# Where four weight pieces land, and in which order the last products run, in a four-layer attention and feed-forward kernel

## The chip, the core and the metric

The kernel runs on one core of one Trainium2 chip. The metric is the device time of one execution in microseconds (us); the time before is the median of four runs. A core has five engines, each with an instruction stream of its own: PE (TensorE, matrix products), DVE (VectorE), ACT (ScalarE), POOL (GpSimd) and SP (SyncE). SP, and for some transfers ACT and POOL, issue the DMAs. [...] PE reads SBUF and writes PSUM, the accumulator memory; DVE and ACT read results from there.

## The reference, cut to what matters

The input `x` has 4 batches of 256 tokens of 256 numbers, in float32. Four layers follow; each adds a cross-attention on 512 context tokens, and then a feed-forward part:

```python
x = x + xattn_L(layernorm(x), ctx)       # L = 1..3: 16 heads of 128, 8 kv heads
x = x + ffn_L(layernorm(x))
# layer 1's ffn: 8 experts of width 176, each token goes to 2, and a shared expert
# layer 3's ffn, for each batch b:
weights = x @ W_r + b_r                           # one number for each token
topk_vals, topk_idx = top_k(weights, 64)
h   = gelu(x[topk_idx] @ W1 + b1)                 # 64 tokens, 256 -> 1024
blk = h @ W2 + b2                                 # 1024 -> 256
out = scatter(blk * weight) + x * (not selected)
```

Before an attention layer the raw weights Wq, Wk, Wv and Wo are folded, head by head, into two matrices: `m_sb` (Wq with Wk) and `n_sb` (Wv with Wo). Attention then works with these and with the context directly.

## The kernel before, in words

`bounded_path` runs once. PE, ACT, DVE and POOL execute what they are given in the order in which the program is written by hand (`manual_schedule`), so a wait at one instruction holds all that stands behind it on that engine. SP's DMAs are also issued in written order.

**The raw weights of layer 2.** `load_raw(L, i, after)` (line 958) issues four DMAs on SP for piece `i` of 4: `wq` and `wo` of 512 KB, `wk` and `wv` of 128 KB. They land in tiles of the pool `rawp`, which here has 3 buffers. `after` makes each DMA wait for a given instruction. `folding` (line 974) is a generator of eight steps, two for each piece. A step is four products `pm` (L983), one product `pn` (L999), ACT's scaling into `m_sb` (L991) and two squares (L994), and DVE's copy into `n_sb` (L1002). `pm` and `pn` take turns in the PSUM buffers called "mm".

**Around it: layer 1's experts.** Tokens are sorted into 23 blocks of 128 slots. For a block, POOL gathers tokens from DRAM (`xg`), PE turns them and multiplies (`pgu`, `pgT`, `pyr`), ACT copies the result (`yr`, L2315), and SP writes it to DRAM (`yd`, L2316). In the loop over `j`, pieces 0, 1 and 2 of layer 2's weights are issued at `j` = 2, 8 and 14, each behind the `yr` copy of the block just finished. After the loop `load_raw(2, 3)` asks for piece 3. It takes the buffers of piece 0, and so waits until PE has read them in the first two fold steps. Then come the rest of the shared expert (`psh`, `pysh`), the eight fold steps, and `Back`: 16 gathers by POOL (`yg`, L2325), two for each half batch, of which 12 are issued in a row and four later; DVE adds them to `x` (L2333). Layer 2's first queries (`pq`, L1765) follow.

**The last output of an attention layer.** For the last batch, `last_output` (line 1889) multiplies head pairs 4 to 7 with `n_sb`, in one PSUM tile `py` of 2 chunks of 128 tokens (L1896): 16 products, 32 entries of the trace, head pair outside, chunk inside. DVE then adds both chunks to `x` (L1904). The four head pairs are divided by their softmax sums just before, two on POOL and two on DVE (L1860). DVE also finishes the other half of the output (`w`, L1793 to L1796, and L1887) before L1904. After it come `Norm` (L917 to L920: statistics on DVE, a power on POOL) and the feed-forward part.

**The end.** Layer 3's feed-forward part routes each batch in stages (`Router`: `weights`, `spread`, `places`, `gathered`, `rest`). `rise3` computes `ph` and the gelu (L2697, L2704), `fall3` computes `po` (L2712) and `blk` (L2716), and `put(b)` sends a batch's 64 rows back to their tokens (`py`, L2722), adds them (L2726) and issues the output (L2727). `blk` holds two batches on its 128 partitions: rows 0 to 63 are the even batch, rows 64 to 127 the odd one. Batches 0 to 2 are raised together, the last one for itself.

Of the kernel before, what the change touches and what calls it, by code (L numbers as in the profile page):

```python
# [9 lines left out]
F32 = mybir.dt.float32  # L10
# [3 lines left out]
ALU = mybir.AluOpType  # L14
# [3 lines left out]
P = 128  # L18
B, S, D = 4, 256, 256
NC = S // P  # L20
ND = D // P
SK, DC = 512, 128
NK = SK // P
H, G = 16, 8
# [13 lines left out]
KSEL = 64  # L38
# [797 lines left out]
def bounded_path(ctx: ExitStack, tc: tile.TileContext, t, out: bass.AP, over):  # L836
# [70 lines left out]
    class Norm:  # L907


        def __init__(self, b, name):  # L910
            self.b, self.name = b, name
            st = small.tile([P, NC, 6], F32, tag="ln_st", name=f"st_{name}")
            self.mv = small.tile([P, NC, 2], F32, tag="ln_mv", name=f"mv_{name}")
            ve = small.tile([P, NC], F32, tag="ln_ve", name=f"ve_{name}")
            self.rstd = small.tile([P, NC], F32, tag="ln_rstd", name=f"rstd_{name}")
            for c in range(NC):
                nc.vector.bn_stats(st[:, c, :], x_sb[b][:, c, :])  # L917
                nc.vector.bn_aggr(self.mv[:, c, :], st[:, c, :])
            nc.vector.tensor_scalar(ve, self.mv[:, :, 1], LN_EPS, None, ALU.add)
            nc.gpsimd.tensor_tensor(self.rstd, ve, neghalf[:, :NC], ALU.pow)  # L920
# [34 lines left out]

    raws = {}

    def load_raw(L, i, after=None):

        wq, wk, wv, wo = (t[f"L{L}_{n}"] for n in ("wqT", "wkT", "wvT", "wo"))  # L960
        h0, g0 = 4 * i, 2 * i
        wq_t = rawp.tile([P, 4, D], F32, tag="wq_t", name=f"wq_{L}_{i}")
        wk_t = rawp.tile([P, 2, DC], F32, tag="wk_t", name=f"wk_{L}_{i}")
        wv_t = rawp.tile([P, 2, DC], F32, tag="wv_t", name=f"wv_{L}_{i}")
        wo_t = rawp.tile([P, 4, D], F32, tag="wo_t", name=f"wo_{L}_{i}")
        for dst, src, a, z in ((wq_t, wq, h0, 4), (wk_t, wk, g0, 2), (wv_t, wv, g0, 2), (wo_t, wo, h0, 4)):
            dma = nc.sync.dma_start(dst, src[a * P : (a + z) * P, :].rearrange("(h e) d -> e h d", e=P))
            if after:
                behind(dma, after)
        raws[L, i] = wq_t, wk_t, wv_t, wo_t  # L970
# [711 lines left out]

    NB = S // 32 * 2

    def attention(L, m_sb, n_sb, first_xnT=None, after=None, at_end=None):

# [12 lines left out]
        with tc.tile_pool(name=f"att{L}", bufs=2) as ap:  # L1699
# [186 lines left out]
                    x = x_sb[self.b].rearrange("p c (e d) -> p (c e) d", d=P)  # L1886
                    nc.vector.tensor_tensor(x, x, w, ALU.add)  # L1887

            def last_output(b):

                py = bank("s", [P, NC, D], f"py{L}")
                for hp in range(H // 4, H // 2):
                    o = outs.pop((b, hp))
                    for c in range(NC):
                        for j in range(2):
                            nc.tensor.matmul(  # L1896
                                py[:, c, :],
                                lhsT=o[:, j * S + c * P : j * S + (c + 1) * P],
                                rhs=n_sb[:, 2 * hp + j, :],
                                start=(hp == H // 4 and c == 0 and j == 0),  # L1900
                                stop=(hp == H // 2 - 1 and c == NC - 1 and j == 1),
                            )
                for c in range(NC):
                    nc.vector.tensor_tensor(x_sb[b][:, c, :], x_sb[b][:, c, :], py[:, c, :], ALU.add)  # L1904

            xnTs[0] = first_xnT if first_xnT is not None else layernorm(0, f"a{L}_0")[1]
            first_queries(0)
# [45 lines left out]
            out.add()  # L1953
            if at_end:
                at_end()
            last_output(B - 1)

# [147 lines left out]
    with tc.manual_schedule(engines={E.PE, E.Activation, E.DVE, E.Pool}):  # L2105
        with (
# [492 lines left out]
    class Router:  # L2599


        def __init__(self, b):
            self.b = b
            self.norm = Norm(b, f"f3_{b}")

        def weights(self):
            b = self.b
# [100 lines left out]
    def fall3(i, k0, k1):  # L2708
        if k0 == 0:
            po3[i] = bank("o", [P, D], f"po3_{i}")  # L2710
        for k in range(k0, k1):
            nc.tensor.matmul(  # L2712
                po3[i], lhsT=hT[:, k, i * P : (i + 1) * P], rhs=w32[:, k, :], start=(k == 0), stop=(k == F3 // P - 1)
            )
        if k1 == F3 // P:
            nc.vector.tensor_tensor(blk[:, i, :], po3[i], b32, ALU.add)  # L2716

    def put(b):
        i, r0 = b // 2, KSEL * (b % 2)
        for c in range(NC):  # L2720
            py = bank("mm", [P, D], f"py3_{b}_{c}")
            nc.tensor.matmul(  # L2722
                py, lhsT=pickT[r0 : r0 + KSEL, i, c, :], rhs=blk[r0 : r0 + KSEL, i, :], start=True, stop=True
            )
            xc = x_sb[b][:, c, :]
            nc.vector.scalar_tensor_tensor(xc, py, wts[:, b, c : c + 1], xc, ALU.mult, ALU.add)  # L2726
            (nc.scalar if c and b >= 2 else nc.sync).dma_start(out[b, c * P : (c + 1) * P, :], xc)  # L2727

    routers = {}

# [20 lines left out]
    with tc.manual_schedule(engines={E.PE, E.Activation, E.DVE, E.Pool}):  # L2751

        pr = bank("t", [P, ND, P], "pwr")
        nc.vector.memset(ones_s, 1.0)
        for d in range(ND):
            wide = tile3b("diag", [P, NC, P], f"wr{d}")
            nc.vector.tensor_copy(wide[:, 0, :], wr[:, d : d + 1].to_broadcast([P, P]))
            nc.tensor.matmul(pr[:, d, :], lhsT=wide[:, 0, :], rhs=ident, start=True, stop=True)
        nc.vector.tensor_copy(wrb, pr.rearrange("p d q -> p (d q)"))

        def end3():
            nc.scalar.preload_act_table_set("gelu_apprx_tanh_and_others")
            routers[2].gathered()
            routers[2].rest()

        attention(3, *mn, first_xnT=xnT3, after=beside3, at_end=end3)
# [4 lines left out]
        last = Router(B - 1)  # L2771
# [95 lines left out]
```

## Time and profile before

| | |
|---|---|
| median of 4 runs | 1497.68 us |
| the four runs | 1497.06, 1490.90, 1498.69, 1498.29 us |
| the profiled execution | 1499.73 us, span 1497.5 us |
| PE busy in the span | 1453.5 us (97%) |
| DVE, POOL, ACT busy | 895.8, 663.8, 573.4 us |
| mean granted PE clock | 0.987 |

The span is the time between the first and the last record of the profiled execution; 2.2 us of its time lie around it. A line of the timeline gives a start, a length, the engine, the line of the kernel, the operation, out<-in, the shapes and a count, and in brackets how long the engine had been idle and what released it. Where several instructions are merged, the length runs from the first start to the last end. "SPq", "ACTq" and "POOLq" are an engine's instruction queue, which issues DMAs. A table of windows gives for each stretch its length, the busy time of PE, PE's weight loads, DVE, ACT and POOL with counts, the granted PE clock, the share of the DMA engines and GB/s.

### The profile page before, as it was taken

What the parts mean: (1) busy time and instruction counts of PE and PEld (TensorE: products, weight loads), DVE (VectorE), ACT (ScalarE), POOL (GpSimd) and SP (SyncE); (2) the same over time, 40 slices, a digit from 0 to 9 for tenths busy, and PEclk for the clock granted to TensorE, in tenths of its full rate; (3) what the DMA queues carried; (4) which work ended last, traced back from release to release, by engine and by line L of the source; (5) the groups of instructions that cost most, each with busy time, mean ns of one, the idle gap of its engine ahead of it and who ended that gap; (6) DMA issues with size and microseconds to landing.
All of it is one profiled execution on the core that took longest, in us unless ns stands there. A gap on an engine that the chain in (4) does not pass through costs nothing.

```text
span 1497.5 us, 19706 instructions
## 1 busy us (share of the span) xinstructions
PE 1453.5 (97%) x7287; PEld 946.0 (63%) x7287; DVE 895.8 (60%) x1940; ACT 573.4 (38%) x1100; POOL 663.8 (44%) x778
## 2 busy tenths in 40 slices
PE   8999999999999999998999999999999999999997
PEld 7665577565566666665556666665886566666666
DVE  5566774566666556522566655656445666767674
ACT  4556443433433333233543333333224433333331
POOL 2122232476555454233356556556003665455560
PEclk8899999999999999999999999999999999999999
DMA  5000031110000001154110000000310000000000
GB/s 162 2 1 2 12 95 36 67 41 0 7 1 8 1 1 50 45 175 129 43 36 1 1 1 1 1 1 0 106 36 29 31 1 1 1 0 1 1 1 31
DMA packets 40036, 43.36 MB, mean 29 GB/s; under 512 B 3897, under 2 KB 36890, under 8 KB 39932
## 3 DMA queue, kind: packets, MB, share of 16 engines
q1 hardware_dynamic: 36956, 35.85, 7.5%
q0 software_dynamic: 1872, 5.11, 1.2%
q8 instruction: 60, 0.98, 0.3%
q10 hardware_dynamic: 1104, 1.05, 0.2%
q14 instruction: 44, 0.36, 0.1%
HBM read 36.89 MB, written 5.11 MB: 28 GB/s over the span
## 4 chain that ended last, share of the span: by engine, by line
PE 90%; DVE 6%; POOL 2%; issue 1%; ACT 1%; another core or an unknown queue 0%; POOLq 0%; ACTq 0%; DVEq 0%
PE ps L1813 22%; PE po L1819 21%; PE paq L1783 5%; PE pao L1783 4%; PE pbq L1783 4%; PE pbo L1783 3%; PE ph L2476 2%; PE po L2513 2%; PE pgu L2286 2%; PE po L1329 2%; PE ps L1319 2%; PE pyf L1446 2%; PE py L1896 1%; PE paf L1396 1%; PE pn L999 1%; PE pm L983 1%
## 5 line engine op out<-in xcount | busy, mean ns | idle before, releaser
L1826 POOL TENSOR_TENSOR half<-pT 128x1024 f32<-128x1024 f32 x96 | 225.8, 2352 | 383.2 <-ACT pT L1816 333.3
L1813 PE MATMUL ps<-qT,cT 128*128 128x512 f32 x768 | 345.6, 593 | 0.4 <-ACT qT L1770 0.4
L1819 PE MATMUL po<-pT,c_sb 128*128 128x512 f32 x768 | 345.2, 592 | 0.0
L1816 ACT ACTIVATE pT<-ps,mbias 128x512 f32<-128x512 f32 x384 | 263.8, 687 | 163.9 <-PE ps L1813 153.9
L1819 PEld LDWEIGHTS po<-pT,c_sb 128*128 128x128 f32 x768 | 145.9, 190 | 183.7 <-issue 183.7
L1813 PEld LDWEIGHTS ps<-qT,cT 128*128 128x128 f32 x768 | 138.7, 190 | 138.6 <-issue 137.3
L1823 ACT COPY oT<-po 128x512 f32<-128x512 f32 x96 | 56.2, 586 | 263.6 <-PE po L1819 263.6
L1860 POOL TENSOR_TENSOR oT<-oT,wide 128x512 f32<-128x512 f32 x90 | 115.4, 1302 | 26.2 <-DVE wide L1859 26.2
L1323 ACT ACTIVATE pT<-ps 128x512 f32<-128x512 f32 x128 | 66.1, 603 | 46.5 <-PE ps L1319 46.3
L1793 DVE TENSOR_TENSOR qT<-qT,paq 128x128 f32<-128x128 f32 x90 | 25.5, 284 | 90.8 <-ACT qT L1792 90.7
L1832 DVE TENSOR_TENSOR half<-half 128x512 f32<-128x512 f32 x96 | 72.1, 751 | 10.1 <-POOL half L1826 10.1
L1834 DVE STREAM_TRANSPOSE turned<-half 128x512 f32<-128x512 f32 x96 | 68.3, 712 | 6.3
L1793 DVE TENSOR_TENSOR w<-w,pao 128x128 f32<-128x128 f32 x21 | 6.0, 286 | 109.9 <-ACT w L1792 109.9
L1783 PEld LDWEIGHTS paq<-xnT_a,m_sb 128*128 128x128 f32 x360 | 58.0, 191 | 21.5 <-PE po L1819 10.5
L1783 PE MATMUL paq<-xnT_a,m_sb 128*128 128x128 f32 x360 | 70.7, 278 | 0.1
L1783 PE MATMUL paq<-xx,m_x 128*128 128x128 f32 x360 | 69.8, 275 | 0.0
L1838 DVE TENSOR_REDUCE sums<-turned 128x16 f32<-128x512 f32 x96 | 65.9, 686 | 3.4
L1783 PE MATMUL pao<-n_x,ox 128*128 128x128 f32 x336 | 65.0, 275 | 0.0
L1859 DVE STREAM_TRANSPOSE wide<-rz 128x512 f32<-128x512 f32 x96 | 62.2, 686 | 0.1
L1792 ACT COPY qT<-paq 128x128 f32<-128x128 f32 x90 | 23.9, 265 | 85.2 <-PE paq L1783 83.1
L1796 DVE TENSOR_TENSOR qT<-qT,pbq 128x384 f32<-128x384 f32 x90 | 49.9, 554 | 9.4
L1783 PEld LDWEIGHTS paq<-xx,m_x 128*128 128x128 f32 x360 | 54.7, 192 | 0.0
(392 smaller groups left out, 2603.7 us busy)
## 6 DMA issues: line engine op xcount, KB each, us to landing
wo<-in_L_wo SPq DMA_DIRECT2D x13, 512.0 KB
wq<-in_L_wqT SPq DMA_DIRECT2D x12, 512.0 KB
yd<-yr SPq DMA_DIRECT2D x23, 128.0 KB
w<-in_F_w SPq DMA_DIRECT2D x4, 512.0 KB
wgu<-in_F_wgT SPq DMA_DIRECT2D x2, 880.0 KB
wgu<-in_F_wuT SPq DMA_DIRECT2D x2, 880.0 KB
wk<-in_L_wkT SPq DMA_DIRECT2D x12, 128.0 KB
wv<-in_L_wvT SPq DMA_DIRECT2D x12, 128.0 KB
```

The lines of the kernel that those rows point to most:

```text
L1323: nc.scalar.activation(pT[kp][:, j], ps[j], AF.Exp)
L1783: nc.tensor.matmul(p[:, at, :], lhsT=lhsT, rhs=rhs, start=(k == 0 and at == 0), stop=(k == len(of) - 1 and i == which[-1]),)
L1813: nc.tensor.matmul(ps, lhsT=cT[:, b, k * P : (k + 1) * P], rhs=qT, start=True, stop=True)
L1816: nc.scalar.activation(pT[:, k, :], ps, AF.Exp, bias=mbias[:, b, k : k + 1])
L1819: nc.tensor.matmul(po, lhsT=c_sb[:, b, k, :], rhs=pT[:, k], start=(k == 0), stop=(k == NK - 1))
L1823: done["head"] = nc.scalar.copy(raw, po).ins
L1826: nc.gpsimd.tensor_tensor(half, pT[:, 0:2], pT[:, 2:4], ALU.add)
L1832: nc.vector.tensor_tensor(part, half[:, 0], half[:, 1], ALU.add)
L1834: nc.vector.transpose(turned.rearrange("p f i -> p (f i)"), part)
L1838: nc.vector.tensor_reduce(sums[b, hp // 4][:, hp % 4, :], turned, AX.X, ALU.add)
L1859: nc.vector.transpose(wide, rzs[b, hp // 4][:, hp % 4, :, None].to_broadcast([P, NB, 32]))
L1860: eng.tensor_tensor(outs[b, hp], outs[b, hp], wide.rearrange("p f i -> p (f i)"), ALU.mult)
```

## The change

There are three groups of edits.

First, layer 2's four weight pieces are all issued within the loop over blocks, at `j` = 1, 5, 9 and 13. Piece 0 no longer lands in `rawp`, but in parts of `m_sb` and `n_sb` that belong to heads 8 to 15, which the fold writes only in its second half. Pieces 1, 2 and 3 take the three buffers, and nothing is issued after the loop.

Second, in `last_output` the chunk is the outer loop. DVE adds a chunk as soon as its eight products are there, and in layer 3 takes its statistics too (`Norm.chunk`). This holds for layers 1, 2 and 3, since all use `last_output`.

Third, the end of layer 3 is reordered: `routers[2].rest()` moves from the end of attention to behind `last.places()`; parts of `fall3(0, ...)` are put between the last batch's stages; `put` takes a pair of batches, changes between the two halves of the 128 rows from one product to the next, and uses the four "s" buffers instead of the two "mm" ones.

As built, the changed kernel has PE's first product of the second chunk wait for DVE in all three layers. In layer 1, three of the shared expert's products (`psh`) stand between the two chunks; in layers 2 and 3 nothing does.

```diff
-    def load_raw(L, i, after=None):
+    def load_raw(L, i, after=None, tiles=None):
...
-        wq_t = rawp.tile([P, 4, D], F32, tag="wq_t", name=f"wq_{L}_{i}")
-        wk_t = rawp.tile([P, 2, DC], F32, tag="wk_t", name=f"wk_{L}_{i}")
-        wv_t = rawp.tile([P, 2, DC], F32, tag="wv_t", name=f"wv_{L}_{i}")
-        wo_t = rawp.tile([P, 4, D], F32, tag="wo_t", name=f"wo_{L}_{i}")
+        if tiles is None:
+            tiles = [
+                rawp.tile(shape, F32, tag=f"{n}_t", name=f"{n}_{L}_{i}")
+                for n, shape in (("wq", [P, 4, D]), ("wk", [P, 2, DC]), ("wv", [P, 2, DC]), ("wo", [P, 4, D]))
+            ]
+        wq_t, wk_t, wv_t, wo_t = tiles
...
-                if j in (2, 8, 14):
-                    load_raw(2, j // 6, done["slots"])
-            load_raw(2, 3)
-            mn = folded(2)
+                if j == 1:
+
+                    mn = folded(2)
+                    load_raw(
+                        2, 0, done["slots"],
+                        (mn[1][:, 8:12, :], mn[0][:, 1, 12:14, :], mn[0][:, 1, 14:16, :], mn[1][:, 12:16, :]),
+                    )
+                if j in (5, 9, 13):
+                    load_raw(2, j // 4, done["slots"])
...
-            def last_output(b):
+            def last_output(b, chunk=None):
...
-                for hp in range(H // 4, H // 2):
-                    o = outs.pop((b, hp))
-                    for c in range(NC):
+                for c in range(NC):
+                    for hp in range(H // 4, H // 2):
                         for j in range(2):
                             nc.tensor.matmul(
                                 py[:, c, :],
-                                lhsT=o[:, j * S + c * P : j * S + (c + 1) * P],
+                                lhsT=outs[b, hp][:, j * S + c * P : j * S + (c + 1) * P],
                                 rhs=n_sb[:, 2 * hp + j, :],
-                                start=(hp == H // 4 and c == 0 and j == 0),
-                                stop=(hp == H // 2 - 1 and c == NC - 1 and j == 1),
+                                start=(hp == H // 4 and j == 0),
+                                stop=(hp == H // 2 - 1 and j == 1),
                             )
-                for c in range(NC):
                     nc.vector.tensor_tensor(x_sb[b][:, c, :], x_sb[b][:, c, :], py[:, c, :], ALU.add)
+                    if chunk:
+                        chunk(c)
...
-    def put(b):
-        i, r0 = b // 2, KSEL * (b % 2)
+    def put(i):
+
         for c in range(NC):
...
+            for b in (2 * i + 1, 2 * i):
+                r = slice(KSEL * (b % 2), KSEL * (b % 2 + 1))
+                py = bank("s", [P, D], f"py3_{b}_{c}")
+                nc.tensor.matmul(py, lhsT=pickT[r, i, c, :], rhs=blk[r, i, :], start=True, stop=True)
...
-        rise3(range(0, 5), 0, 3 * KSEL)
+        rise3(range(0, 6), 0, 3 * KSEL)
         last.weights()
-        rise3(range(5, 6), 0, 3 * KSEL)
+        fall3(0, 0, 2)
         last.spread()
         rise3(range(6, NK3), 0, 3 * KSEL)
-        fall3(0, 0, 4)
+        fall3(0, 2, 4)
         last.places()
-        fall3(0, 4, NK3)
+        routers[2].rest()
+        fall3(0, 4, 6)
         last.gathered()
+        fall3(0, 6, NK3)
+        picked(1)
         last.rest()
-        picked(1)
+        rise3(range(NK3), 3 * KSEL, 4 * KSEL)
         put(0)
-        rise3(range(NK3), 3 * KSEL, 4 * KSEL)
+        fall3(1, 0, NK3)
         put(1)
-        fall3(1, 0, NK3)
-        put(3)
-        put(2)
```

More of the change, by code (lines that the diff above doesn't have):

```diff
@@ L907, in bounded_path, with __init__ @@
     class Norm:
-        def __init__(self, b, name):
+        def __init__(self, b, name, by_chunk=False):
             self.b, self.name = b, name
@@ L915, in __init__, with chunk @@
             self.rstd = small.tile([P, NC], F32, tag="ln_rstd", name=f"rstd_{name}")
-            for c in range(NC):
[L917 to L920, printed above, removed]
+            self.st, self.ve = st, ve
+            if not by_chunk:
+                for c in range(NC):
+                    self.chunk(c)
+        def chunk(self, c):
+            nc.vector.bn_stats(self.st[:, c, :], x_sb[self.b][:, c, :])
+            nc.vector.bn_aggr(self.mv[:, c, :], self.st[:, c, :])
+            if c == NC - 1:
+                nc.vector.tensor_scalar(self.ve, self.mv[:, :, 1], LN_EPS, None, ALU.add)
+                nc.gpsimd.tensor_tensor(self.rstd, self.ve, neghalf[:, :NC], ALU.pow)
         def tokens(self, keep=None):
@@ L1683, in bounded_path, with attention @@
     NB = S // 32 * 2
-    def attention(L, m_sb, n_sb, first_xnT=None, after=None, at_end=None):
+    def attention(L, m_sb, n_sb, first_xnT=None, after=None, at_end=None, chunk=None):
         with tc.tile_pool(name=f"att{L}", bufs=2) as ap:
@@ L1887, in add @@
                     nc.vector.tensor_tensor(x, x, w, ALU.add)
-            def last_output(b):
+            def last_output(b, chunk=None):
                 py = bank("s", [P, NC, D], f"py{L}")
-                for hp in range(H // 4, H // 2):
-                    o = outs.pop((b, hp))
-                    for c in range(NC):
+                for c in range(NC):
+                    for hp in range(H // 4, H // 2):
                         for j in range(2):
@@ L1897, in last_output @@
                                 py[:, c, :],
-                                lhsT=o[:, j * S + c * P : j * S + (c + 1) * P],
+                                lhsT=outs[b, hp][:, j * S + c * P : j * S + (c + 1) * P],
                                 rhs=n_sb[:, 2 * hp + j, :],
-                                start=(hp == H // 4 and c == 0 and j == 0),
-                                stop=(hp == H // 2 - 1 and c == NC - 1 and j == 1),
+                                start=(hp == H // 4 and j == 0),
+                                stop=(hp == H // 2 - 1 and j == 1),
                             )
-                for c in range(NC):
                     nc.vector.tensor_tensor(x_sb[b][:, c, :], x_sb[b][:, c, :], py[:, c, :], ALU.add)
+                    if chunk:
+                        chunk(c)
             xnTs[0] = first_xnT if first_xnT is not None else layernorm(0, f"a{L}_0")[1]
@@ L1955, in attention @@
                 at_end()
-            last_output(B - 1)
+            last_output(B - 1, chunk)
     NBLK = (B * S * 2 + NE * (P - 1)) // P
@@ L2599, in bounded_path, with __init__ @@
     class Router:
-        def __init__(self, b):
+        def __init__(self, b, by_chunk=False):
             self.b = b
-            self.norm = Norm(b, f"f3_{b}")
+            self.norm = Norm(b, f"f3_{b}", by_chunk)
         def weights(self):
@@ L2716, in fall3 @@
             nc.vector.tensor_tensor(blk[:, i, :], po3[i], b32, ALU.add)
-    def put(b):
-        i, r0 = b // 2, KSEL * (b % 2)
+    def put(i):
         for c in range(NC):
[L2721 to L2727, printed above, removed]
+            for b in (2 * i + 1, 2 * i):
+                r = slice(KSEL * (b % 2), KSEL * (b % 2 + 1))
+                py = bank("s", [P, D], f"py3_{b}_{c}")
+                nc.tensor.matmul(py, lhsT=pickT[r, i, c, :], rhs=blk[r, i, :], start=True, stop=True)
+                xc = x_sb[b][:, c, :]
+                nc.vector.scalar_tensor_tensor(xc, py, wts[:, b, c : c + 1], xc, ALU.mult, ALU.add)
+                (nc.scalar if c and i else nc.sync).dma_start(out[b, c * P : (c + 1) * P, :], xc)
     routers = {}
@@ L2759, in bounded_path @@
         nc.vector.tensor_copy(wrb, pr.rearrange("p d q -> p (d q)"))
+        last = Router(B - 1, by_chunk=True)
         def end3():
@@ L2763, in end3 @@
             routers[2].gathered()
-            routers[2].rest()
-        attention(3, *mn, first_xnT=xnT3, after=beside3, at_end=end3)
+        attention(3, *mn, first_xnT=xnT3, after=beside3, at_end=end3, chunk=last.norm.chunk)
         NK3 = F3 // P
@@ L2770, in bounded_path @@
         blk = f3t.tile([P, B // 2, D], F32, tag="blk", name="blk")
-        last = Router(B - 1)
-        rise3(range(0, 5), 0, 3 * KSEL)
+        rise3(range(0, 6), 0, 3 * KSEL)
         last.weights()
-        rise3(range(5, 6), 0, 3 * KSEL)
+        fall3(0, 0, 2)
         last.spread()
         rise3(range(6, NK3), 0, 3 * KSEL)
-        fall3(0, 0, 4)
+        fall3(0, 2, 4)
         last.places()
-        fall3(0, 4, NK3)
+        routers[2].rest()
+        fall3(0, 4, 6)
         last.gathered()
+        fall3(0, 6, NK3)
+        picked(1)
         last.rest()
-        picked(1)
+        rise3(range(NK3), 3 * KSEL, 4 * KSEL)
         put(0)
-        rise3(range(NK3), 3 * KSEL, 4 * KSEL)
+        fall3(1, 0, NK3)
         put(1)
-        fall3(1, 0, NK3)
-        put(3)
-        put(2)
 def tile_cross_attention_blocks(tc: tile.TileContext, t, out: bass.AP):
```

## The prediction

> **What bounds the kernel now.** I read the page's busy shares and its chain first. They say that the kernel is one long row of matrix products: an edit pays only where PE stands still or runs at a lower clock.
>
> ```profile
> PE 1453.5 (97%) x7287; PEld 946.0 (63%) x7287; DVE 895.8 (60%) x1940; ACT 573.4 (38%) x1100; POOL 663.8 (44%) x778
> PE 90%; DVE 6%; POOL 2%; issue 1%; ACT 1%; another core or an unknown queue 0%; POOLq 0%; ACTq 0%; DVEq 0%
> ```
>
> PE is idle for 44 us in all. The list of PE's waits has one long entry, 6.5 us in the fold of layer 2's weights; everything else is 3.4 us or less. So I opened the timeline there.
>
> ```profile
> 702.57 0.38 SPq L967 DMA_DIRECT2D wq<-in_L_wqT  x1
> ...
> 703.23 1.16 PE L983 MATMUL pm<-wk,wq 128*128 128x128 f32 x8 [0.33 <-issue]
> ...
> 704.22 1.02 PE L999 MATMUL pn<-wo,wv 128*128 128x512 f32 x2
> ...
> 707.89 0.95 POOL L2325 DMA_INDIRECT yg<-yd,where  x1 [0.30 <-issue]
> 708.93 0.42 DVE L2155 TENSOR_TENSOR x_sb<-x_sb,pysh 128x256 f32<-128x256 f32 x1 [5.62 <-remote]
> 711.09 0.60 ACT L991 ACTIVATE m_sb<-pm 128x512 f32<-128x512 f32 x1 [6.98 <-remote]
> ...
> 711.74 2.08 PE L983 MATMUL pm<-wk,wq 128*128 128x128 f32 x8 [6.50 <-ACT m_sb L991]
> ```
>
> PE's products of 703.23 should be through at about 704.4, yet ACT starts on them at 711.09, DVE starts on an older result at 708.93, and the profile names no engine that released either ("remote"). PE waits for ACT. These are the only "remote" waits of the span. They lie where piece 3 (1.31 MB, issued from 702.57) meets the 12 gathers of `Back`; the DMA view has the last of that traffic before 711. The windows show what follows the wait:
>
> ```profile
> 705.00:708.00 3.00, 0.24 (x1) 0.00 (x0) 0.00 (x0) 0.00 (x0) 2.09 (x4) 1.00 1.05 344
> 708.00:711.70 3.70, 0.00 (x0) 0.00 (x0) 0.98 (x2) 0.60 (x1) 0.83 (x1) 0.77 0.59 193
> 711.70:714.00 2.30, 2.26 (x9) 2.21 (x10) 0.89 (x3) 1.05 (x5) 0.00 (x0) 0.50 0.00 0
> 714.00:717.00 3.00, 3.00 (x11) 1.98 (x10) 1.40 (x4) 1.36 (x5) 0.00 (x0) 0.53 0.00 0
> ```
>
> The DMA engines are full, PE is empty, and afterwards PE has half its clock until 717.
>
> **Part one, the weight pieces.** The change takes the only bulk transfer out of this window. The wait is 6.50 us. The slow clock costs more: three groups (`pm`, `pn`, `pm`) take 2.08, 1.91 and 1.79 us, where the same groups at full clock take 1.06, 1.02 and 1.06, so 2.64 us. Together 9.1 us. What is late next is DVE: its order puts two `yg` adds (0.88 us), the norm (1.36), POOL's power (0.7) and `xn` (0.74) ahead of the fifth step's `n_sb` copy. Step by step with these durations and without the wait, `pm` of the fourth step starts at 704.7, DVE's statistics end at 709.7 (POOL's last early gather ends at 708.84, so it does not hold the power), `xn` ends at 711.3, that copy at 712.0, `pm` of the seventh step follows at 712.0. From there to `pq` the trace takes 4.5 us (720.60 to 725.12): `pq` at 716.6 and not 725.12, a gain of **8.5 us**. Bounds: 9.1 if DVE keeps up; 0 if the gathers alone hold back PE's results. They might: already the products that end at 700.75 reach ACT only at 702.58, before piece 3 is issued. I take 8.5, because the delay grew from 1.8 to 6.7 us when the bulk data came.
>
> The moved DMAs: four times four issues between blocks instead of three times four. Four issues hold SP for 2.3 us (634.56 to 636.88), and the `yd` writes queue behind them; `yr` has three buffers, so three blocks of 2.84 us, 8.5 us, cover that. Behind the data stands the `xg` gather, issued four blocks ahead (11.4 us) against some 4 us for 1.31 MB (0.33 MB in each of the microseconds 705 to 708). PE is busy 20.00 of 20 us from 640 to 660 with a piece in flight, so I cost it at nothing; without cover it would be up to 6.5 us for each piece. POOL's queue is not passed. Landing in `m_sb` and `n_sb` adds waits to two DVE copies for data that landed 40 us earlier: nothing.
>
> **Part two, the last output by chunks.** The products and their 7.17 us stay. What moves is when PE needs which divided head pair, and the new wait: PE's second chunk waits for DVE's add of the first, and all of PE's stream stands behind it. Layer 2:
>
> ```profile
> 1047.01 7.17 PE L1896 MATMUL py<-n_sb,oT 128*128 128x256 f32 x32 [0.27 <-POOL oT L1860]
> ...
> 1048.21 1.27 POOL L1860 TENSOR_TENSOR oT<-oT,wide 128x512 f32<-128x512 f32 x1 [1.25 <-DVE wide L1859]
> ...
> 1051.69 0.69 DVE L1887 TENSOR_TENSOR x_sb<-x_sb,w 128x512 f32<-128x512 f32 x1
> ...
> 1054.23 0.75 DVE L1904 TENSOR_TENSOR x_sb<-x_sb,py 128x256 f32<-128x256 f32 x2 [1.84 <-PE py L1896]
> ```
>
> A head pair and chunk is 7.17/8 = 0.9 us. After two pairs (1048.8) PE needs the third, which POOL finishes at 1049.48: with 0.27 for the signal it goes on at 1049.75, and the chunk ends at 1051.5. DVE is busy until 1052.4 with `w` and L1887, adds the chunk in 0.4, and the second chunk runs from 1052.95 to 1056.6. Before, PE was through at 1054.18: **+2.4 us**, with nothing in the 10 us behind it that gives it back. Layer 1, by the same rows (584.83; POOL at 587.29; DVE until 590.2): the first chunk ends at 589.3, the three `psh` products (4.9/8 = 0.61 each) fill the wait until 591.2, and only the 1.0 us for the third pair remains, with 0.1 for `xn`, which comes 1.4 later: **+1.1**. Layer 3: start 1458.68, POOL at 1460.74, first chunk through at 1462.7, DVE until 1463.8 (without the 1.04 us of `rest`, which has moved), add until 1464.2, second chunk until 1467.8 and not 1465.8: **+2.1**. An idle PE of 1.80 us (579.6 to 581.4) left the clock at 1.00, so I add nothing for it. Bounds for the three together: 2.3 (only the wait for the third pair in each) to 7.
>
> The trace of before has no read of half a `py` while PE writes the other half, so no row says whether it needs a wait. [...]
>
> **Part three, the end.**
>
> ```profile
> 1470.98 0.68 PE L2624 MATMUL pw<-diag,ones 128*128 128x128 f32 x4 [1.27 <-DVE diag L2617]
> ...
> 1478.68 1.13 PE L2722 MATMUL py<-blk,pickT 64*128 64x256 f32 x4
> ...
> 1488.74 2.40 PE L2722 MATMUL py<-blk,pickT 64*128 64x256 f32 x8 [0.52 <-DVE blk L2716]
> ...
> 1490.75 0.92 DVE L2726 SCALAR_TENSOR_TENSOR x_sb<-py,wts,x_sb 128x256 f32<-128x256 f32 x2 [0.36 <-PE py L2722]
> ```
>
> With the first chunk's add and statistics done early, DVE needs 4.4 us (5.2 before) from the end of `py` to `diag`: 1472.4. PE gets there after six rises (4.06) and a quarter of `fall3` (0.93), at 1472.8: the 1.27 us wait goes. The 0.39 before `ppick` goes too, since two more falls stand ahead of it. `put(0)` is 2.1 us before (twice 1.05). Opposite halves can share PE: the page's L1319, on 16 rows in four groups, does 16 entries of 256 columns in 1.15 us (0.07 each) against 0.26 here. I take half, 0.13, so 1.05 less; bounds 0 and 1.5. New waits, for `pick` and for the last gelu's buffer, some 0.2. At the very end four adds follow each other without the 0.36 us pause: 0.3. Sum **-2.8**. `rest` of batch 2 (1.04 us on DVE) now lies beside `pxg` and falls; uncovered it would cost that.
>
> **Sum.** -8.5 + 2.4 + 1.1 + 2.1 - 2.8 = -5.7 us. Against the profiled execution, 1499.73 to 1494.0. That execution lies 2.05 above the median, so I forecast 1497.68 - 5.7 = **1492.0**. The run at 1490.90 lies about 7 below the three others, as if the wait had been absent; then the change would give 1490.9 + 2.8 = 1493.7, still within this case.
>
> **The rivals.** *The wait stays* (1500.5): the 12 gathers, not piece 3, hold back PE's results; then only +5.6 - 2.8 is left, and the kernel is slower, decided where more than 5.7 of the 8.5 us stay at the fourth `pm`. For it: the early 1.8 us. Against it: gathers go on all through the block loop without such a wait. *The waits cost less* (1489): all 9.1 gained, chunk waits of 4.1 where DVE is half a microsecond earlier in each layer, halves overlapping fully and no new wait at the end (-1.27 - 0.39 - 1.5 - 0.3 = -3.5), so -8.5. For it: each lies within its bounds. *The hold-up moves into the block loop* (above 1505): piece loads meet gathers there four times, and two waits of 6.5 come on top. Against it: three pieces did so before, and PE never waited. *The chunks do not do what they say*, since PE stops for DVE: that is in my sum.
>
> **How the numbers follow.** About 0.5%, 7.5 us, is what a measurement of this kernel can tell from no change: below 1490.2 or above 1505.2. Forecast 0.54, of which 0.12 below 1490.2 (its own range is 1489 to 1495.5); waits cost less 0.20, all faster; wait stays 0.20, of which 0.02 above 1505.2; hold-up in the loop 0.06, slower. Faster 0.32, same 0.60, slower 0.08. The range 1486.5 to 1501.5 leaves out the loop case and the tails of the others.
>
> **What would show it.** Right: no "remote" wait between 695 and 715, clock 1.00 there, `pq` some 8 us earlier after the blocks; PE idle about 2 us in the middle of `py` in layers 2 and 3, released by DVE's add; `pw` without a wait. Wrong: a wait of several us at the fourth `pm` with no bulk DMA, PE waits for `xg` or `yr` in the block loop, or chunks that follow each other without a gap.

## The result, and the profile after

| | before | after |
|---|---|---|
| median | 1494.56 us (78 runs, 1490.56 to 1499.73) | 1497.38 us (52 runs, 1493.39 to 1503.99) |
| ratio, 95% interval | | 1.0022, 1.0014 to 1.0030 |
| the profiled executions | 1499.73 us, clock 0.987 | 1493.92 us, clock 0.991 |

The kernel became some 3 us slower, within the 0.5% that I had called no change; the forecast was 5.7 us faster. The two profiled executions say the opposite, -5.8 us. So I cut both spans at the same products of PE:

| stage, by its first and last product | before | after | difference | forecast |
|---|---|---|---|---|
| start to the first `pq` of layer 1 | 259.80 | 250.81 | -8.99 | 0 |
| to layer 1's `py` | 325.03 | 325.03 | 0 | 0 |
| to `plist` (layer 1's `py` and what follows) | 28.78 | 29.78 | +1.00 | +1.1 |
| `plist` to the first `pxg` | 9.27 | 10.95 | +1.68 | 0 |
| the loop over blocks | 68.00 | 68.00 | 0 | 0 |
| the fold: first `psh` after the blocks to `pq` | 34.23 | 33.66 | -0.57 | -8.5 |
| to layer 2's `py` | 321.90 | 321.90 | 0 | 0 |
| layer 2's `py` to the next `pm` | 30.90 | 33.39 | +2.49 | +2.4 |
| to layer 3's `py` | 380.77 | 380.79 | 0 | 0 |
| layer 3's `py` to the first `ph` | 6.96 | 9.10 | +2.14 | +2.1 |
| `ph` to the end | 31.81 | 28.49 | -3.32 | -2.8 |

The first row is no work of the change. The windows of the first 50 us, before and then after, show the same busy time at another clock:

```profile
0.00:50.00 50.00, 44.26 (x252) 35.56 (x256) 22.94 (x49) 18.26 (x35) 10.13 (x34) 0.80 0.38 122
```

```profile
0.00:50.00 50.00, 44.26 (x348) 34.34 (x348) 28.63 (x65) 23.88 (x47) 13.64 (x35) 0.93 0.40 122
```

PE had 252 matrix products done there before, 348 after. The row of 1.68 is the clock too: 3.4 us at half clock, which the same code shows in some executions and not in others. What is left is +1.00 - 0.57 + 2.49 + 2.14 - 3.32 = +1.74 us, a little under the interval of the ratio (2.1 to 4.5 us); where the rest lies, one pair of executions does not say. The last row contains a stretch that no edit steers: from DVE's last add until the outputs have landed, runs of the same code took 5.1 to 7.0 us. Up to DVE's last add the end took 26.02 us before and 22.23 after, 3.79 less, and in all kernels with the changed end and the early statistics it was 22.22 or 22.23. Only the fold missed its forecast by much. The timeline of after, there:

```profile
693.37 1.06 PE L991 MATMUL pm<-m_sb,n_sb 128*128 128x128 f32 x8
...
695.13 1.46 PE L2159 MATMUL pysh<-wds,gsT 128*128 128x256 f32 x6
...
696.05 0.60 ACT L999 ACTIVATE m_sb<-pm 128x512 f32<-128x512 f32 x1 [1.95 <-PE pn L1007]
...
696.70 1.16 PE L991 MATMUL pm<-wk,wq 128*128 128x128 f32 x8
...
701.32 0.95 POOL L2333 DMA_INDIRECT yg<-yd,where  x1 [0.30 <-issue]
701.70 0.42 DVE L2163 TENSOR_TENSOR x_sb<-x_sb,pysh 128x256 f32<-128x256 f32 x1 [3.54 <-remote]
704.55 0.60 ACT L999 ACTIVATE m_sb<-pm 128x512 f32<-128x512 f32 x1 [6.96 <-remote]
704.60 0.69 DVE L1010 COPY n_sb<-pn 128x512 f32<-128x512 f32 x1 [2.47 <-remote]
...
705.20 2.07 PE L991 MATMUL pm<-wk,wq 128*128 128x128 f32 x8 [5.86 <-ACT m_sb L999]
```

The "remote" waits and PE's wait for ACT are still there. Three results of PE, through at 694.43, 696.59 and 697.86, are taken up at 696.05, 701.70 and 704.55: 1.6, 5.1 and 6.7 us late. In the trace it is the signals (the updates of the semaphore that PE's products raise and that ACT and DVE wait for here) that come late, not the products: the updates that go with these three stand at 696.03, 701.68 and 704.53. The next one, for the `pn` that was through at 699.35, stands at 704.57, only 0.04 us later, though a `pn` takes 1.02 us. Over the whole trace the median update of this semaphore comes 0.01 us after a product's end. And the windows there, from 698.4 to the end of the wait, have no bulk data:

```profile
698.40:701.40 3.00, 0.95 (x2) 0.12 (x2) 0.00 (x0) 0.00 (x0) 2.09 (x4) 0.99 0.32 97
701.40:705.20 3.80, 0.00 (x0) 0.00 (x0) 1.02 (x2) 0.61 (x2) 0.86 (x1) 0.50 0.23 69
```

The DMA engines are busy for a quarter to a third (97 and 69 GB/s, the gathers alone), where before they were full (a share of 1.05, 344 GB/s from 705 to 708). Layer 2's last output, and then the end:

```profile
1040.13 1.99 PE L1903 MATMUL py<-n_sb,oT 128*128 128x256 f32 x8 [0.27 <-POOL oT L1868]
...
1042.64 1.99 PE L1903 MATMUL py<-n_sb,oT 128*128 128x256 f32 x8 [0.52 <-POOL oT L1868]
...
1045.60 0.42 DVE L1910 TENSOR_TENSOR x_sb<-x_sb,py 128x256 f32<-128x256 f32 x1
1046.07 3.72 PE L1903 MATMUL py<-n_sb,oT 128*128 128x256 f32 x16 [1.44 <-DVE x_sb L1910]
```

```profile
1468.17 0.61 PE L2637 MATMUL pw<-diag,ones 128*128 128x128 f32 x4
...
1477.90 1.17 PE L2737 MATMUL py<-blk,pickT 64*128 64x256 f32 x8
...
1483.24 1.13 PE L2737 MATMUL py<-blk,pickT 64*128 64x256 f32 x8 [0.52 <-DVE blk L2729]
1483.97 1.66 DVE L2739 SCALAR_TENSOR_TENSOR x_sb<-py,wts,x_sb 128x256 f32<-128x256 f32 x4 [0.79 <-PE py L2737]
```

In the first, PE stops for the third pair (0.52 us) and, before the second chunk, for DVE's add (1.44). In the second, `pw` has no wait, eight entries of the returning product take 1.13 to 1.17 us where four took 1.13, and DVE's four adds follow each other.

### The profile page after: what moved, and what is told of

Read it like the earlier page. It is cut to its first block, busy times and chain, and to the rows that moved or that the text cites. A ratio compares the mean times of both kernels' runs of the same rounds, so it can differ in the third digit from the quotient of the medians.

```text
span 1491.9 us, 19703 instructions
## 1 busy us (share of the span) xinstructions
PE 1444.5 (97%) x7287; PEld 938.4 (63%) x7287; DVE 896.0 (60%) x1940; ACT 573.1 (38%) x1100; POOL 664.4 (45%) x778
## 3 DMA queue, kind: packets, MB, share of 16 engines
q10 hardware_dynamic: 1104, 1.05, 0.2%
## 4 chain that ended last, share of the span: by engine, by line
PE 89%; DVE 7%; POOL 2%; issue 1%; ACT 1%; another core or an unknown queue 0%; DVEq 0%; ACTq 0%; POOLq 0%
PE ps L1821 22%; PE po L1827 21%; PE paq L1791 5%; PE pao L1791 4%; PE pbq L1791 4%; PE pbo L1791 3%; PE ph L2489 2%; PE po L2526 2%; PE pgu L2294 2%; PE ps L1327 2%; PE po L1337 2%; PE pyf L1454 2%; PE paf L1404 1%; PE pn L1007 1%; PE pm L991 1%; PE psh L2138 1%
```

## The experiments

The first theory was that POOL's 12 gathers in a row, and not the bulk data, hold back PE's signals. Its rivals: the bytes that arrive ("traffic"), or something else at this place of the program ("place"). The runs took place on four chips, here A to D; that mattered more than I knew. In all of them the stages that an edit did not touch kept their lengths, except where PE's clock was halved and in the stretch after the last add, so I compare stages.

**Chip B, first look.** Plain DMAs in place of the gathers:

```diff
 for i in range(2):
+    if n < N8 - 2:
+        nc.sync.dma_start(self.y[:, i, :], yd[(2 * n + i) * P : (2 * n + i + 1) * P, :])
+        continue
     nc.gpsimd.indirect_dma_start(
```

> Edit on the changed kernel: the 12 gathers that POOL issues in a row before the fold of layer 2 become 12 plain DMAs of the same 131 KB each, issued by SP; they bring rows of yd in storage order instead of each token's rows (that choice of rows is left out). Measure: the fold stage, from the first psh after the block loop to the first pq of layer 2, 34.24 us before and 33.66 us after the change, with a wait of 5.86 us at the fourth pm. Theory 'row of gathers' (POOL's indirect gathers in a row, from about the sixth on, hold back PE's signals until some 2 us after the last): no wait, full clock, so 33.7 less 5.9 less 1.6 of slow clock (pm and pn 2.07 and 1.57 where 1.06 and 1.02 are normal) = 26.2 us. Theory 'traffic' (1.5 MB that arrive in SBUF in this stretch hold PE back, whoever issues them): a wait of several us stays, stage above 31 us. Theory 'place' (something else at this place, such as fetched instructions or ACT's table): the wait stays as it is, 33.7 us.

Measured: fold 25.27 us, no wait, but the run tests nothing. SP's order is not fixed by hand, against what I wrote at the start; its loads moved up into the loop over blocks, where the `yd` writes queued behind them and the loop took 74.91 us.

Twelve gathers moved to the end of the fold, and four rows of four:

```diff
-for n in range(N8 - 2):
+for n in range(NC):
     backs[n] = Back(n)
...
+for n in range(NC, N8):
+    backs[n] = Back(n)
```

This is the first of the two edits; its late twelve are added to `x` in units 0, 2 and 4 of attention.

> Edit on the changed kernel: four of the 16 gathers stay before the fold (batch 0), the other 12 are issued in a row at the end of the fold, beside the start of layer 2's attention, and added there. Theory 'row of gathers': the wait moves with the row. The fold takes about 26 us and not 33.7, and PE meets a new wait of 5 to 7 us in the first 20 us of layer 2's attention, from about the sixth gather of the row to some 2 us after the last; from the first psh after the blocks to layer 2's last py it takes within 3 us of the 355.6 us of the changed kernel (33.66 + 321.90). Theories 'traffic' and 'place': 'traffic' says the same as 'row'; 'place' says that the wait stays at the fourth pm of the fold (33.7 us) and that attention keeps its 321.9 us.

> Edit on the changed kernel: the same 16 gathers in four rows of four: batch 0 before the fold, batch 1 after the fourth fold step, batches 2 and 3 in units 1 and 3 of layer 2's attention, where DVE adds them two units later. Theory 'row of gathers' (a row of five or fewer holds nothing back): no wait in the fold, 26.2 us and not 33.66, and no new wait in attention (321.9 us, at most 1 us more for POOL's 8 issues of 1.25 us beside its other work), so the span falls by 6.5 to 7.5 us against the changed kernel at equal clock elsewhere. Theory 'traffic' (bytes per us): the gathers of a row come at the same rate, so each row of four holds PE back by a part, fold 28 to 33 us. Theory 'place': 33.7 us.

Measured: the fold took 24.77 us in both. From there to layer 2's last `py` it was 321.24 us with the late row, so there was no new wait, and 324.15 with rows in units 1 and 3, where PE waits in all 1.6 us for POOL's `oT` and `ox`. The wait goes with the row, but does not come back with it.

Two PSUM tiles, in chunk order:

```diff
-py = bank("s", [P, NC, D], f"py{L}")
+pys = [bank("s", [P, D], f"py{L}_{c}") for c in range(NC)]
```

> Edit on the changed kernel: in last_output each chunk has a PSUM tile of its own, in two of the s buffers, instead of halves of one. Theory 'shared tile' (PE's second chunk stands still until DVE has added the first, because both lie in one tile): the waits of 1.44 us and what stands before them go, and only the wait for the third head pair is left (0.52 us in layers 1 and 2, 0.16 in layer 3). From py to the next stage's first product: layer 2 (py to the first pm of layer 3's fold) 30.9 before, 33.4 after, here 31.4; layer 3 (py to the first ph of the last rise) 6.96 before, 9.10 after, here 7.2; layer 1 (py to the fourth psh group) 24.98 before, 25.99 after, here 25.5. Rival (PE waits for DVE whatever the tile, since the third pair and DVE's order set it): 33.4, 9.1 and 26.0 as they are.

Measured: layer 1 28.68 to `plist`, layer 2 31.68, layer 3 7.39. DVE's wait is gone: sharing one tile cost 1.71 us in each of layers 2 and 3. Layer 1's 1.1 us less are not the tile's: PE was at half clock from 572.1 to 575.5, just before `py`, and so came late enough to find the third pair ready. But the same trace has the unmoved row of 12, and this:

```profile
698.55 1.15 PE L991 MATMUL pm<-wk,wq 128*128 128x128 f32 x8
...
701.68 0.94 POOL L2333 DMA_INDIRECT yg<-yd,where  x1 [0.30 <-issue]
```

The fourth `pm` starts without a wait while the row still runs; fold 25.27. So the row alone is not enough, and the two runs with moved gathers say nothing of it.

**Chip A, both kernels again.**

> The kernel before, once more and unchanged, for its trace. In the run with two PSUM tiles the fold of layer 2 took 25.27 us with all 12 gathers in a row and not one late signal, against 34.23 in the first trace of before and 33.66 in that of the changed kernel. Theory 'execution' (the hold-up of PE's signals belongs to some executions, or to how they were recorded: in both early traces two thirds of the gathers' landing records are missing, in the later ones none): here no 'remote' wait, fold 25 to 26 us with piece 3 and the gathers in it. Theory 'kernel' (bulk data or gathers hold PE back in this kernel's order): fold 34.2 again.

> The changed kernel, once more and unchanged. Theory 'execution': fold 25.3 us here, like the run with two PSUM tiles, and the same as before's within 1 us, so that part one is worth nothing in such executions; the stages of last_output and of the end as in the first trace (layer 1 12.6 to pxn, layer 2 33.4, layer 3 9.1 and 28.5), so about +0.9 + 2.5 + 2.1 - 3.3 = 2.2 us against before, ratio 1.0015. Theory 'kernel': fold 33.7 again, ratio 1.002.

Measured: fold 34.23 and 33.69, the wait is back, every stage within 0.4 us of the first traces; ratio of after 1.0017 (0.9998 to 1.0036). So it seems to depend on the chip. The nearest pair is the two-tile run on B (fold 25.27) and the mixed order below on A (33.75), whose code differs only in `last_output`. No one kernel with the row was traced on both kinds of chip, so "with the same kernels" in the expectation for the late row says too much. The 39 gathers of a run (23 of blocks, 16 of `Back`) leave 16 landing records each. In the four traces of A 356 to 394 of these 624 exist, in this one of B 622. Before's fastest run is 1491.06 us on A (23 runs), and its one run on B 1487.33.

Part two undone, and a mixed order on two tiles:

```diff
-for c in range(NC):
-    for hp in range(H // 4, H // 2):
+h1, h2, h3 = H // 4, H // 4 + 2, H // 2
+for hps, c in (((h1,), 0), ((h1,), 1), ((h1 + 1,), 0), ((h1 + 1,), 1), ((h2, h3 - 1), 0), ((h2, h3 - 1), 1)):
+    for hp in hps:
```

> Edit on the changed kernel: last_output in its old order again (head pair outside, chunk inside, one tile, DVE's two adds after the last product); pieces and the end stay changed. By the stages: layer 1 11.7 us to pxn and not 12.6, layer 2 30.9 and not 33.4, layer 3 7.0 to the first ph and not 9.1; the end loses some of its gain, since DVE starts the last batch's statistics after both adds: 28.5 to 29.3 us from the first ph to the end, against 28.5 and 31.8 before. Sum: 5 us below the changed kernel, 2.5 to 3.3 below before, ratio 0.998. Rival (the end needs the early statistics): the end goes back to 31 us, and the kernel is at before's time.

> Edit on the changed kernel: two PSUM tiles, one for each chunk, and an order in which PE needs the third head pair no earlier than before: pairs 5 and 6 of the eight for both chunks, then the last two pairs for chunk 0, then for chunk 1. Theory 'shared tile': no wait for the third pair and none for DVE; layer 1 11.3 to 11.7 us to pxn, layer 2 30.9, layer 3 7.0 to the first ph, end 28.3; sum 2.5 + 2.1 + 0.9 = 5.5 us below the changed kernel, 3.5 below before, ratio 0.9975. Rival (DVE's other sums in that stretch set PE's pace whatever the order): layer 2 31.7 and layer 3 7.4 as in the run with two tiles in chunk order.

Measured: the old order has ratio 0.998 (0.9966 to 0.9993), layer 2 30.90, layer 3 6.96, and 29.41 to the end (23.05 to the last add). The mixed order has 0.9966 (0.9949 to 0.9983), 30.90, 6.96 and 28.25 (22.22 to the last add); so the early statistics are worth 0.8 us of the end. In the mixed order PE's row is whole again, and DVE's first add lies inside it:

```profile
1044.74 7.17 PE L1904 MATMUL py<-n_sb,oT 128*128 128x256 f32 x32 [0.27 <-POOL oT L1868]
...
1050.23 0.42 DVE L1913 TENSOR_TENSOR x_sb<-x_sb,py 128x256 f32<-128x256 f32 x1
```

**Chip C, where the wait shows: does it go with the gathers?** The late row with the mixed order; plain DMAs held behind the last block (`behind(dma, done["slots"])`); six gathers early and ten late; rows of four again.

> Edit: the changed kernel with the last output in the mixed order on two tiles, and with 12 of the 16 gathers moved from before the fold of layer 2 to its end, beside the start of layer 2's attention (batch 0's four stay). Runs so far: the wait at the fourth pm showed in all traces of one chip (fold 33.7 to 34.2 us) and in none of another (24.8 to 25.3), with the same kernels. Theory 'row on a slow chip' (where it shows, it is the row of gathers that holds back PE's signals, from about the sixth on): on such a chip the fold takes 25 us, and the wait either moves into the first 20 us of attention (then the time is that of the mixed order, 1491.8 and ratio 0.9966) or meets no PE signal that is needed at once (then 8 us less: about 1484, ratio 0.991). Theory 'place on a slow chip' (the wait belongs to this place in the program, not to the gathers): fold 33.7 us, ratio 0.9966. On a chip without the wait: fold 24.8, attention 321.2, ratio about 0.997.

> Edit on the changed kernel: the 12 gathers in a row before the fold become 12 plain DMAs of the same 131 KB by SP, now held behind the last block's yr copy, so that they run beside the fold as the gathers did (which rows they bring is left out, they come in storage order). On a chip that shows the wait: theory 'gathers by POOL' (the many small writes or POOL's issues hold PE's signals): fold 25 to 26 us; theory 'bytes' (1.5 MB into SBUF): a wait of several us remains, above 30 us; theory 'place': 33.7. On a chip without the wait: 25 us by all three.

> Edit on the changed kernel: six gathers in a row before the fold and ten at its end. On a chip that shows the wait, theory 'row' (from about the sixth gather on signals come late, until some 2 us after the last): at most one signal is late by up to 2 us, fold 25 to 27 us; theory 'place': 33.7 us. On a chip without it: 25 us.

> The kernel of the run with four rows of four gathers once more, in case this chip shows the wait, which that one did not. On such a chip, theory 'row': fold 24.8 us and no late signal, attention of layer 2 324.2 us as there; theory 'bytes': fold 28 us or more; theory 'place': 33.7. On a chip without the wait: as before, 24.8 and 324.2.

| | fold | to layer 2's `py` |
|---|---|---|
| chip A, after | 33.69 | 321.92 |
| late row of 12 | 24.77 | 328.74 |
| plain DMAs | 25.27 | 321.89 |
| six, then ten | 25.27 | 324.71 |
| rows of four | 26.46 | 325.58 |

The late row takes the wait along, into attention, with the same mark:

```profile
721.57 0.95 POOL L2335 DMA_INDIRECT yg<-yd,where  x1 [0.30 <-issue]
721.91 0.59 ACT L1778 COPY qT<-pq 128x512 f32<-128x512 f32 x1 [6.40 <-remote]
...
724.72 2.42 ACT L1824 ACTIVATE pT<-ps,mbias 128x512 f32<-128x512 f32 x4 [2.22 <-remote]
725.46 5.43 PE L1827 MATMUL po<-pT,c_sb 128*128 128x512 f32 x8 [5.45 <-ACT pT L1824]
```

The plain DMAs bring as many bytes (but other rows of `yd`) beside the first steps of the fold and hold nothing; DVE takes up a product 0.04 us after its end:

```profile
694.48 6.53 SPq L2334 DMA_DIRECT2D yg<-yd  x12
...
699.78 1.12 PE L1007 MATMUL pn<-n_sb,m_sb 128*128 128x512 f32 x2
...
700.94 0.69 DVE L1010 COPY n_sb<-pn 128x512 f32<-128x512 f32 x1 [1.75 <-PE pn L1007]
```

So it is neither the place nor the traffic. A row of six holds up no product in the fold; the ten that follow cost 1.8 + 1.1 us of PE's time. The rows of four have PE's waits of chip B to a tenth; what their stages are longer (1.7 and 1.4 us) is PE at half clock for 3.4 us in each. The late row's ratio is 0.9962 (0.9947 to 0.9977).

**The rows of four where POOL has time, with and without piece 3.** Rows before the fold, after its fourth step, in unit 0 of batch 0 and in unit 0 of batch 1; mixed order. The second kernel has part one undone.

```diff
         if b == 0:
             load_waiting(1 if hp < 4 else 5)
+            if hp == 0:
+                for k in (4, 5):
+                    backs[k] = Back_of[0](k)
+            if hp == 2:
+                for k in (4, 5):
+                    backs[k].add()
+        if b == 1:
...
```

> Edit: the changed kernel with the last output in the mixed order on two tiles, and the 16 gathers in four rows of four: before the fold, after its fourth step, and in the first units of batch 0 and of batch 1 of layer 2's attention, each added two units later. Theory 'row' (a row of four holds nothing back; the 2.2 us that rows in units 1 and 3 cost in attention came from POOL's own work there): fold 24.8 us, attention 321.3 to 322.5, so 8 to 9 us less than the changed kernel there on a chip that shows the wait, and with the mixed order's 5.5 some 14 below the changed kernel and 11 to 12.5 below before: ratio 0.992 to 0.9925; on a chip without the wait ratio 0.997. Rival (rows of four hold signals back too, or POOL is late for the sums of unit 1): attention 324 to 326, ratio 0.994.

> The same with part one undone: pieces 0, 1 and 2 at j = 2, 8 and 14, piece 3 after the loop into the buffers of piece 0, so that its 1.31 MB arrive in the middle of the fold. Theory 'row' (the gathers alone held PE back, the bulk data nothing): fold within 0.6 us of the 24.8 of the other kernel of this call. The prediction's theory (the bulk data where gathers run hold PE back): a wait of 2 us or more at a pm of the fold. Rival (the last two steps wait for piece 3 to land): the seventh step's pm waits for the DMA.

Measured, on chip D: fold 24.77 and 24.76, to `py` 321.28 in both, all 624 records, no wait; the ratio of the first is 0.9968 (0.9953 to 0.9983). No kernel with the long row was traced on D, but before itself runs at 1481.92 to 1490.51 us there (17 runs), lower than on A and C, so D most likely does not show the wait. I ran the pair once more.

> The kernel of e12_best again, unchanged. If this chip shows the wait (before's runs lie at 1491 to 1500 there, at 1482 to 1490.5 on a chip without it): theory 'row': fold 24.8 us and attention 321.3 to 322.5, no hold-up of several us, so the kernel loses nothing against the chip without the wait while before loses 9: ratio 0.9905 to 0.992. Rival (rows of four hold signals too): fold or attention 2 to 5 us longer, ratio 0.993 to 0.9965. If it does not: 0.997 again.

> The kernel of e13_piece3 again, unchanged: piece 3 arrives in the middle of the fold. On a chip that shows the wait: theory 'row': fold 24.8 to 25.5 us. The prediction's theory (bulk data beside gathers hold PE back): a wait of 2 us or more at a pm of the fold, fold above 27 us. On a chip without it: 24.8.

Measured, on chip C, which showed the wait: fold 24.77 in both, to `py` 321.30 and 321.29; ratio of the first **0.991 (0.9891 to 0.993)**, 1481.58 us against 1494.72. Piece 3 arrives in the middle of the fold, between two rows of gathers. The windows of the second kernel:

```profile
700.00:703.00 3.00, 3.00 (x17) 2.22 (x15) 1.11 (x2) 1.46 (x6) 0.00 (x0) 1.00 0.70 214
703.00:706.00 3.00, 3.00 (x19) 2.22 (x18) 2.16 (x5) 2.53 (x10) 0.00 (x0) 1.00 0.67 223
```

214 and 223 GB/s arrive, PE is busy for every microsecond at full clock. The bulk data cost nothing, and part one is worth nothing here. POOL issues no gather in these windows; what bulk data add beside the long row is read from before and after, at most 0.57 us. The first kernel of the pair lies below before by 0.3% on D and by 0.9% on C; the changed kernel, not run there, lay above it on A. The first kernel takes 1482.87 us on D and 1481.58 on C, while before takes 1487.71 and 1494.72: without a long row the two chips are alike, and with it C is 7 us slower. On C alone, the late row of 12 takes 1490.80 us, and 1481.58 where only the gathers are placed otherwise, in rows of four.

## Why the prediction was right and wrong

**The step that failed** is the choice within part one's bounds: "I take 8.5, because the delay grew from 1.8 to 6.7 us when the bulk data came". The delay grows alike without them, 1.6 to 5.1 to 6.7 us: it grows along the row of gathers, and the data came in the middle of that row by chance of the order. The right bound was the lower, 0 ("0 if the gathers alone hold back PE's results"); measured 0.57. The warning stood in my own text, the result taken late at 702.58 before piece 3 was issued. I set against it that gathers go on through the block loop without a wait, but one in 2.84 us is not twelve at 1.25 us.

**The size of that term was right.** With the wait gone the fold takes 25.27 us in the order of the changed kernel, 8.4 less than its 33.66 with the wait; the prediction's 8.5 off 34.23 would be 25.73. Before's medians on D and A lie 8.0 us apart (1487.71 and 1495.73), though chance of the clock is in that difference too.

**The rival that held** is "the wait stays", in its mechanism and its sum: +2.8 us against the reference, measured +2.8 between the medians. I gave it 0.20. That the sum fits to the tenth is luck: the stages give +1.74, since parts one and three gained half a microsecond each beyond the rival's terms. Its decision point, more than 5.7 of the 8.5 us left at the fourth `pm`, is met by 5.86 us of wait.

**Part two** held term by term: +1.00, +2.49, +2.14 for +1.1, +2.4, +2.1. In layer 2 I had the second chunk start 5.94 us after the first (1052.95 - 1047.01); it did, at 1046.07 - 1040.13. PE did stand still for the shared tile (1.44 us in layer 2), and the run with two tiles (31.68 us there and not 33.39) shows that this, and not DVE's load, was the reason. No run let PE write one half while DVE reads the other, so whether that is allowed stays open here.

**Part three**: -3.32 for -2.8, and -3.79 up to the last add, where the scatter of the outputs' landing is left out. The waits at `pw` (1.27) and `ppick` (0.39) went as worked out. The products of `put(0)` and `put(1)` took 2.26 us and now take 1.17: 1.09 for 1.05. That is 0.15 us for an entry, near the 0.13 that I took and far from the 0.07 of the upper bound; two opposite halves together take about the time of one. The tail from `blk` to the last add fell from 2.98 to 2.45: 0.53 for 0.3. The 0.2 for new waits did not come. These four give 3.28 of the 3.79; most of the rest is that `pw` and `ppick` add 0.23 and 0.22 us less to PE's busy time when no wait stands before them, which I had not counted.

**The moved DMAs**: block loop 68.00 in both, nothing, as costed. So the rival "hold-up moves into the block loop" fell.

**The step from the profiled execution to the median** rested on a doubtful reading: I took the run at 1490.90 for one without the wait. The traces show another source of steps between runs, the clock: 249.5 to 259.9 us to layer 1's first `pq`, with no code changed there, and half-clock stretches elsewhere. The profiled 1499.73 us with the shorter start of after (8.99 less) would be 1490.74, with the wait in it. No trace of the run at 1490.90 exists, so this is not shown.

## What to carry to other kernels

A wait that the profile puts down to no engine has to be tied to a resource by moving one suspect at a time: that two things meet in the trace made me price one and trust the other. Cut two traces at the same products before comparing spans; here 9 us of start hid the sign of the change. Repeat a kernel on a second chip before a wait's absence is credited to an edit. And do not break up a reader's tile without giving each part a tile of its own: the mixed order on two tiles gave what the chunk order was after, without its 5.6 us.

## What the runs showed of the hardware

- On three sets of traces (the first ones, chip A, chip C) ten or more indirect gathers that POOL issued 1.25 us apart held back PE's signals by up to 6.7 us, until about 2.3 us after the last gather's end (702.27 and 704.53 in after, 708.84 and 711.07 in before); in the two traces of B with a row of 12 it held nothing (fold 25.27 us with the row in it, 321.24 to layer 2's `py` with the late row). Rows of four held no signal on B, C and D (PE's longest wait from 684 to 800 was 0.7 us on B and C; on D the fold took 24.77), nor did a row of six on C. DVE's signal to PE was prompt in the middle of the row of 12 in after (`n_sb` through at 698.16, PE's `pn` at 698.22). PE's products were not late by the profile: in after two were through at 697.86 and 699.35, 6.67 and 5.22 us ahead of their signals.
- In every trace of A, of C and of the first ones 22 to 43% of the gathers' landing records were missing (where all 39 gathers ran, 356 to 485 of 624 were there; 364 in before and 399 in after, and of the 16 gathers of `Back` alone 75 and 80 of 256), on B and D at most five. The missing records go with the chip and not with the held signals: on C they were missing in the runs with rows of four too, where nothing was held, and in all these traces already in the loop over blocks (289 of 368 were there in before, 319 in after). Whether the hold-up has to do with recording, the runs don't say. Why chips differ stays open, and so does the price in an execution that nobody records.
- Up to PE's last product its clock was halved for 3.4, 6.8, 10.2 or 13.7 us at a time, one to four times the shortest, mostly in the first 150 us, around `plist` and with the held signals (from 710.0 to 716.8 in before, 701.3 to 708.1 in after), and differently for the same code: from `plist` to the first `pxg` the last kernel took 9.27 us on D and 14.24 on C (and its twin 14.24 on D as well).
